# An S4-style block and a routed feed-forward block on one core: first routed query group moved into the light stage, index stores of the two routings spread, turning matrix and last stores rearranged

## The chip, the cores and the metric

The kernel runs on one core of a Trainium2 chip. The metric is the device time of one execution in microseconds (us). The engines are TensorE (PE, matrix products; PEld loads its weights), VectorE (DVE), ScalarE (ACT), GpSimd (POOL) and SyncE (SP). Each takes its own instructions in order; a DMA is issued from the instruction stream of one of them.

## The reference, cut to what matters

The input is x of shape (8, 2048, 512), float32. Two blocks with a skip connection follow each other:

```python
x = x + ssm(layernorm(x))      # per channel: causal convolution over the sequence,
                               # kernel K[d, l] = sum_n C*B_bar*A_bar**l, plus D*x
x = x + ffn(layernorm(x))

def ffn(x):
    light = light_attn(x)                     # windows of 64, own window and both neighbours
    sq,  iq  = route(x, rt_q,  512)           # 512 query rows of each sequence
    skv, ikv = route(x, rt_kv, 1024)          # 1024 context rows of each sequence
    out = heavy_attn(x[iq], x[ikv], skv)      # 8 heads of 64, rms norm, one null key
    full = broadcast(null_q); full[iq] = out * sq
    return light + full
```

`route` scores every row by a dot product, runs 50 rounds of coordinate descent and takes the top rows. All is float32.

## The kernel before, in words

The rows are 128 tiles of 128 rows, 16 to a sequence. There are three stages, one after the other on PE.

**Stage 1, `ssm_phase`.** The 512 channels are taken as 4 blocks of 128. The results of a block stay on chip (`xb`) and `store` writes them to the array `y`, one store per sequence b, each of 1 MB. The last block's stores cannot hide behind a further block: b = 0 goes out on POOL's queue, b = 1 to 7 on ACT's queue (line 353), and each is made to wait until the one before has landed (line 361, `stored[-1]`).

**Stage 2, `light_phase`.** 32 macro tiles of four row tiles. For the first macro tile the kernel already holds `z` on chip with the rows of each tile in reverse order; `turn(0)` turns them over and transposes them with one product against `flip`, a 128 by 128 matrix with ones on the other diagonal, which POOL makes (lines 721 to 724) with a memset and an affine select. `front(n)` makes the keys (`pp`, line 905; DVE evicts them, line 910), then the queries (evicted by ACT, line 908), then the values (line 918). The list of half steps in `steps()` is an order written out by hand for PE: 256 half steps, two to a row tile, each with scores (`sim`, line 974), exponentials on ACT (984), scaling on DVE (990), transposes (1000), the products `po` (1018), an ACT eviction `ot` (1022) and, once per row tile, the output product `pr` (1027), from which DVE makes `row` (1029) and POOL `nul` (1033). `rows`, `turn` and `front` of later macro tiles are generators of which a piece is run in every half step.

Beside this run the two routings, one for sequences 0 to 3 (group 0) and one for 4 to 7 (group 1). `route` is a generator too, and every half step runs two of its pieces through `between`. It has 144 pieces of arithmetic, then the 128 indirect stores of its results (line 641), two to a piece, then 16 pieces that load the lists back. The stores are queued on POOL behind the latest `nul`, so they run once per row tile (two half steps): eight together while one routing stores, sixteen while both do. Group 0 begins at half step 110 and stores from half step 182 to 213; group 1 begins at 132 and stores from 204 to 235.

**Stage 3, `heavy_phase`.** For each sequence three groups of 512 gathered rows: one of queries, two of keys and values. `fetch(n)` issues four gathers of group n (`xg`) from POOL's queue, `norm(n)` makes `z` from them (statistics on DVE, one power on POOL, line 1251, four scalings on DVE, line 1254), then come 16 transposes (line 1269), their evictions, and 16 products for the queries or keys (line 1286), with 16 more for the values. The heavy attention of a sequence also gathers the light result of its query rows, `bg` (line 1318 calls `gather`, line 1213), on POOL's queue.

Of the kernel before, what the change touches and what calls it, by code (L numbers as in the profile page):

```python
# [8 lines left out]
F32 = mybir.dt.float32  # L9
# [3 lines left out]
ALU = mybir.AluOpType  # L13
# [4 lines left out]
P = 128  # L18
B, L, D = 8, 2048, 512
# [4 lines left out]
NC = D // P  # L24
H, DH, WIN = 8, 64, 64
# [68 lines left out]
def ssm_phase(tc, k, x, log_A, B_param, C, Dp, ys):  # L94
# [10 lines left out]
    with ExitStack() as ctx:  # L105
# [245 lines left out]
        def store(cb, b):  # L351
            last = cb == NC - 1
            eng = nc.scalar if last and b else nc.gpsimd
            for y, c0 in ys[b]:
                c1 = c0 + y.shape[0] // P
                i = eng.dma_start(
                    y.rearrange("(i p) d -> p i d", p=P)[:, :, cb * P : (cb + 1) * P],
                    xbs[cb % 2][:, b * NCK + c0 : b * NCK + c1, :])
            if last:

                if b:
                    tc.add_manual_dep(i.ins, stored[-1].ins.name,
                                      mybir.DependencyInfo(mybir.DependencyClass.Sync,
                                                           mybir.DependencyReason.DATA),
                                      reason="stores in turn")
                stored.append(i)
# [107 lines left out]
def route(tc, k, ps, gi, flat, ix, wt):  # L474
# [160 lines left out]
    for r in range(2):  # L635
        nc.vector.tensor_copy(pair[:, r * GB * NCK : (r + 1) * GB * NCK, 0], rows)
    yield
    for b in range(GB):
        for rb, n in ((b, NQT), (GB + b, NLT)):
            for c in range(rb * NCK, (rb + 1) * NCK):  # L640
                nc.gpsimd.indirect_dma_start(  # L641
                    out=flat[c % NFL], out_offset=bass.IndirectOffsetOnAxis(ap=to[:, c : c + 1],
                                                                            axis=0),
                    in_=pair[:, c, :], in_offset=None, bounds_check=2 * GB * NKV - 1,
                    oob_is_err=False)
                if c % 2:
                    yield
    for b in range(GB):
        for rb, n in ((b, NQT), (GB + b, NLT)):
# [19 lines left out]
NM = L // MTOK  # L669


def light_phase(tc, k, ps, wp, args, x, ys, x1, base, out, between, after):

# [5 lines left out]
    with ExitStack() as ctx:  # L679
# [38 lines left out]

        xf = x.rearrange("b l d -> (b l) d")

        flip = sb.tile([P, P], F32, name="flip", tag="nul")
        nc.gpsimd.memset(flip, 0.0)
        nc.gpsimd.affine_select(flip, flip, [[1, P]], ALU.not_equal, 1.0, base=-(P - 1),
                                channel_multiplier=1)
# [207 lines left out]
        def keys(t):  # L932

            it, j = place(t)
            if t == NTT - 1:
                key = k.zp.tile([P, NC, 4 * WIN], F32, name="tail", tag="z")
                nc.gpsimd.memset(key[:, :, HALO:], 0.0)
                nc.gpsimd.tensor_copy(key[:, :, 0:HALO], it["k"][:, :, MTOK:])
                return key, 0
            return it["k"], P * j + P  # L940
# [108 lines left out]
        def steps():  # L1049
# [27 lines left out]
            for s in range(nst):  # L1077
# [3 lines left out]
                if s == 0 or j == 0:  # L1081
                    run(ahead)
                    run(turning)
                    run(scoring)
                    if n == FIRST - 2:
                        between(group=0)
                    if n == NMT - 1:
                        after()
                    ahead = front(n + 1) if n + 1 < NMT else None
                    beyond = rows(n + 2) if n + 2 < NMT else None  # L1090
                    turning = None
                    scoring = later(n - 2) if n in (2, 3) else None
# [12 lines left out]
                if j == 4 and n + 2 < FIRST:  # L1105
                    run(scoring)
# [15 lines left out]
                    done = t  # L1122
                run(ahead, 1)
            finish(done, ots.pop(done))
            between()

        with tc.manual_schedule(engines={mybir.EngineType.PE}):
# [32 lines left out]
    return ld  # L1160


def heavy_phase(tc, k, ps, wp, loaded, w_out, x1, base, out, lists):


# [6 lines left out]
    scale = DH**-0.5  # L1172
    with ExitStack() as ctx:

        inp = ctx.enter_context(tc.tile_pool(name="he_i", bufs=1, reuse_waits="tile"))
# [32 lines left out]
        groups = [(b, i) for b in range(B) for i in range(NG)]  # L1208
        xgs, zs = {}, {}

        def gather(src, ix, c, tag, bufs, pool=sb):
            t = pool.tile([P, D], F32, name=tag, tag=tag, bufs=bufs)
            nc.gpsimd.indirect_dma_start(
                out=t, out_offset=None, in_=src,
                in_offset=bass.IndirectOffsetOnAxis(ap=ix[:, c : c + 1], axis=0),
                bounds_check=B * L - 1, oob_is_err=False)
            return t

        def fetch(n):

            if n >= len(groups):
# [9 lines left out]
            xgs[n] = [gather(x1, ix, c0 + m, "xg", MT + 1, inp) for m in range(MT)]  # L1231

        def norm(n):

            if n >= len(groups):  # L1240
                return
            xg = xgs.pop(n)
            st = sb.tile([P, MT, 6], F32, name="st", tag="st")
            mv = sb.tile([P, MT, 2], F32, name="mv", tag="mv")
            rs = sb.tile([P, MT], F32, name="rs", tag="rs")
            for i in range(MT):
                nc.vector.bn_stats(st[:, i, :], xg[i])
                nc.vector.bn_aggr(mv[:, i, :], st[:, i, :])
            nc.vector.tensor_scalar(rs, mv[:, :, 1], EPS_LN, 1e-24 / D, ALU.add, ALU.mult)
            nc.vector.tensor_tensor(rs, rs, mv[:, :, 1], ALU.max)  # L1250
            nc.gpsimd.tensor_tensor(rs, rs, k.neghalf[:, :MT], ALU.pow)
            z = zs[n] = inp.tile([P, MT, D], F32, name="z", tag="z", bufs=1)
            for i in range(MT):
                nc.vector.tensor_scalar(z[:, i, :], xg[i], mv[:, i, 0:1], rs[:, i : i + 1],
                                        ALU.subtract, ALU.mult)

        def feed():

            fetch(0)
            norm(0)  # L1260
            fetch(1)
            for n, (b, i) in enumerate(groups):
                it = its[b]
                z = zs.pop(n)
                xt = sb.tile([P, NC, MT * P], F32, name="xt", tag="xt")
                for c in range(NC):
                    pt = ps["tp"].tile([P, MT * P], F32, name="pt", tag="tp")
                    for m in range(MT):
                        nc.tensor.transpose(pt[:, m * P : (m + 1) * P],
                                            z[:, m, c * P : (c + 1) * P], k.ident)  # L1270
                    if c % 2 == 0:
                        nc.vector.tensor_scalar(xt[:, c, :], pt, g[:, c : c + 1], None, ALU.mult)
                    else:
                        nc.scalar.mul(xt[:, c, :], pt, g[:, c : c + 1])
                    if c % 2:
                        yield b - 1
                if i == 0:
                    q = it["q"] = sb.tile([P, NC, NQ], F32, name="q", tag="q")
                elif i == 1:
                    kk = it["k"] = low.tile([P, NC, NKV], F32, name="kk", tag="kk")  # L1280
                ms = slice((i - 1) * MT * P, i * MT * P)
                for f in range(NC):
                    pp = ps["mm"].tile([P, MT * P], F32, name="pp", tag="mm")
                    for c in range(NC):
                        w = wq[:, c, :] if i == 0 else wkf[:, 0, c, :]
                        nc.tensor.matmul(pp, w[:, f * P : (f + 1) * P], xt[:, c, :],  # L1286
                                         start=c == 0, stop=c == NC - 1)
                    if i == 0:
                        nc.scalar.mul(q[:, f, :], pp, scale)
                    else:  # L1290
                        nc.vector.tensor_copy(kk[:, f, ms], pp)  # L1291
# [175 lines left out]
def model(ctx, tc, ins, out, debug=None):  # L1467
# [43 lines left out]
    def after():  # L1511
        loaded.update(heavy_loads(tc, wp, rms_g, w_q_h, w_kv_h, null_kv))

    light_phase(tc, k, ps, wp, (ln_g, ln_b, w_qkv, w_out_l, null_q, rt_q, rt_kv), x, ys, x1, base,
                outf, between, after)
    heavy_phase(tc, k, ps, wp, loaded, w_out_h, x1, base, outf, lists)


# [28 lines left out]
```

## Time and profile before

| | us |
|---|---|
| nine runs, median (lowest to highest) | 4871.77 (4866.91 to 4884.26) |
| profiled execution | 4873.9 |
| its span | 4872.2 |
| PE busy in it | 4517.6 (93%) |
| DVE, ACT, POOL busy in it | 2923.5, 1892.4, 1186.2 |
| last product of stage 1 ends, first product of stage 2 begins | 500.5, 515.0 |
| last product of stage 2 ends, first of stage 3 begins | 3151.5, 3163.2 |

The times of the trace count from the start of the span. A row of the timeline gives start, duration, engine, line, operation, tiles, how many instructions the row joins, and in square brackets for how long the engine had been idle before and what released it.

### The profile page before, as it was taken

How to read it: one execution, taken by the hardware profiler on the slowest of the kernel's cores; microseconds unless marked ns; L12 is line 12 of the kernel's file. 1: busy time of each engine (PE TensorE's matmuls, PEld its weight loads, DVE VectorE, ACT ScalarE, POOL GpSimd, SP SyncE). 2: the span in 40 equal slices, each digit the busy share in tenths (PEclk: the TensorE clock that was granted, in tenths of full speed). 3: DMA queues.
4: the chain of work that ended last, by engine and by line, in shares of the span. 5: the costliest groups of instructions: out<-in, count | busy, mean ns of one | idle time of the engine just before them, and what ended most of it. 6: DMA issues, size and time to landing. Idle time of an engine off the chain costs nothing.

```text
span 4872.2 us, 74936 instructions
## 1 busy us (share of the span) xinstructions
PE 4517.6 (93%) x28312; PEld 2628.0 (54%) x28312; DVE 2923.5 (60%) x6971; ACT 1892.4 (39%) x5069; POOL 1186.2 (24%) x1359
## 2 busy tenths in 40 slices
PE   1788899999999999999999899899999999999987
PEld 1677455555555555555554455445555555555554
DVE  8587578777777766668785344445444444454433
ACT  6988133333333333444332233323333333333333
POOL 5354222222222211000145575211101111011000
PEclk9999999999999999999999899999999999999998
DMA  7398634333333321111121122310000100000000
GB/s 255 113 242 222 204 114 141 115 122 117 122 116 119 109 94 58 62 48 57 49 57 42 38 55 53 88 41 27 31 18 27 31 27 27 22 27 27 12 12 12
DMA packets 270090, 383.96 MB, mean 79 GB/s; under 512 B 61728, under 2 KB 134688, under 8 KB 269728
## 3 DMA queue, kind: packets, MB, share of 16 engines
q1 hardware_dynamic: 214688, 268.45, 17.7%
q0 software_dynamic: 40464, 103.37, 7.3%
q10 hardware_dynamic: 14576, 7.34, 0.5%
q8 instruction: 223, 3.65, 0.3%
q14 instruction: 139, 1.14, 0.1%
HBM read 235.42 MB, written 143.72 MB: 78 GB/s over the span
## 4 chain that ended last, share of the span: by engine, by line
PE 56%; issue 27%; DMA 4%; DVE 2%; POOL 1%; another core or an unknown queue 1%; ACT 1%; POOLq 0%; DVEq 0%; ACTq 0%
PE pp L905 18%; PE pv L918 9%; PE pr L1027 9%; PE po L1018 5%; PE pt L1000 4%; PE sim L974 4%; DMA xg<-x,ix 2%; PE pt L886 1%; DMA y<-xb 1%; PE pv L1302 1%; DMA out_dram<-row,ix 1%; PE pp L1286 1%; PE sim L1337 1%; PE pt L1412 1%
## 5 line engine op out<-in xcount | busy, mean ns | idle before, releaser
L905 PE MATMUL pp<-xt,wqkv 128*128 128x512 f32 x2048 | 936.8, 601 | 0.2 <-ACT q L908 0.2
L905 PEld LDWEIGHTS pp<-xt,wqkv 128*128 128x128 f32 x2048 | 369.3, 190 | 398.2 <-issue 396.6
L1343 DVE TENSOR_REDUCE mx<-sim 128x1 f32<-128x1024 f32 x256 | 312.8, 1222 | 343.6 <-PE sim L1337 196.8
L984 ACT ACTIVATE pe<-sim,nb 128x256 f32<-128x256 f32 x1024 | 471.1, 473 | 51.0 <-DVE nb L979 47.3
L1027 PE MATMUL pr<-wo,ot 128*128 128x512 f32 x1024 | 470.4, 601 | 17.5 <-ACT ot L1022 15.4
L918 PE MATMUL pv<-wqkv,xt 128*128 128x512 f32 x1032 | 476.4, 605 | 3.1 <-issue 3.1
L1022 ACT COPY ot<-po 128x256 f32<-128x256 f32 x256 | 95.3, 372 | 978.7 <-PE po L1018 809.7
L1347 ACT ACTIVATE pe<-sim,nb 128x1024 f32<-128x1024 f32 x256 | 285.3, 1114 | 460.8 <-DVE nb L1344 455.1
L979 DVE TENSOR_REDUCE nb<-sim 128x4 f32<-128x1024 f32 x256 | 312.6, 1221 | 198.0 <-PE sim L974 113.5
L1033 POOL TENSOR_TENSOR nul<-row,nq 128x512 f32<-128x512 f32 x128 | 162.5, 1269 | 930.4 <-DVE row L1029 759.5
L1412 PE MATMUL pt<-ident,pe 128*128 128x128 f32 x2048 | 285.9, 284 | 89.6 <-ACT pe L1347 62.9
L1286 PE MATMUL pp<-xt,wa 128*128 128x512 f32 x768 | 351.3, 602 | 4.6 <-DVE kk L1291 4.6
L1412 PEld LDWEIGHTS pt<-ident,pe 128*128 128x128 f32 x2048 | 234.3, 144 | 173.0 <-ACT pe L1347 88.6
L1415 DVE COPY pw<-pt 128x512 f32<-128x512 f32 x256 | 175.6, 686 | 243.8 <-PE pt L1412 243.1
L1000 PEld LDWEIGHTS pt<-ident,pe 128*128 128x128 f32 x2048 | 239.8, 141 | 139.2 <-issue 138.9
L990 DVE TENSOR_SCALAR pe<-pe,rec 128x256 f32<-128x256 f32 x1024 | 298.3, 354 | 7.7
L918 PEld LDWEIGHTS pv<-wqkv,xt 128*128 128x128 f32 x1032 | 186.7, 190 | 210.8 <-issue 207.6
L1027 PEld LDWEIGHTS pr<-wo,ot 128*128 128x128 f32 x1024 | 186.7, 193 | 207.6 <-issue 186.4
L1018 PE MATMUL po<-pw,v 128*64 128x128 f32 x4096 | 282.8, 279 | 5.6 <-issue 5.1
L1417 ACT COPY pw<-pt 128x512 f32<-128x512 f32 x256 | 149.9, 585 | 349.1 <-PE pt L1412 349.1
L641 POOL DMA_INDIRECT list<-r_pair,r_to x256 | 254.4, 994 | 90.0 <-issue 71.5
L1000 PE MATMUL pt<-ident,pe 128*128 128x128 f32 x2048 | 268.8, 274 | 5.6 <-issue 5.6
(250 smaller groups left out, 7158.7 us busy)
## 6 DMA issues: line engine op xcount, KB each, us to landing
xin<-in_L_attn_x_dram SPq DMA_DIRECT2D x32, 1024.0 KB
x1t<-in_L_attn_x_dram SPq DMA_DIRECT2D x128, 256.0 KB
x<-x1t SPq DMA_DIRECT2D x128, 256.0 KB
x1r<-x SPq DMA_DIRECT2D x128, 256.0 KB
base<-row SPq DMA_DIRECT2D x128, 256.0 KB
out_dram<-nul SPq DMA_DIRECT2D x128, 256.0 KB
y<-xb POOLq DMA_DIRECT2D x21, 1024.0 KB
x1t<-x SPq DMA_DIRECT2D x72, 256.0 KB
```

The costliest lines, as they stand in the source:

```text
L905: nc.tensor.matmul(pp, wqkv[:, c, j * D + f * P : j * D + (f + 1) * P], xt[:, c, WIN:], start=c == 0, stop=c == NC - 1)
L918: nc.tensor.matmul(pv[0:m], xt[:, c, s * P : s * P + m], wqkv[:, c, 2 * D :], start=c == 0, stop=c == NC - 1)
L979: dve = nc.vector.reduce_max(nb, sim.rearrange("p a b c -> p (a b) c"), axis=AX.X, negate=True)
L984: act = nc.scalar.activation(pe[:, i, :], sim[:, i // 2, i % 2, :], AF.Exp, bias=nb[:, i : i + 1], accum_out=sums[:, i : i + 1])
L990: nc.vector.tensor_scalar(pe[:, i, :], pe[:, i, :], rec[:, i : i + 1], None, ALU.mult)
L1000: nc.tensor.transpose(pt[:, par, kb, :], self.pe[:, 2 * par + pr, kb * P : (kb + 1) * P], k.ident)
L1018: nc.tensor.matmul(po[64 * par : 64 * par + 64, pr, :], vs[kb][:, h * DH : (h + 1) * DH], self.pw[pr][:, par, kb, :], start=kb == 0, stop= ...
L1027: nc.tensor.matmul(pr, ot[:, c, :], wo[:, c, :], start=c == 0, stop=c == NC - 1)
L1286: nc.tensor.matmul(pp, w[:, f * P : (f + 1) * P], xt[:, c, :], start=c == 0, stop=c == NC - 1)
L1343: nc.vector.reduce_max(mx, sim[:, par, :], axis=AX.X, negate=True)
L1347: nc.scalar.activation(pe, sim[:, par, :], AF.Exp, bias=self.nb[:, h : h + 1], accum_out=self.sums[:, h : h + 1])
L1412: nc.tensor.transpose(pt[:, i, :], pes[half][:, kb * P : (kb + 1) * P], k.ident)
```

## The change

- `store`: the last block's store b waits for the one of b - 2, so that two are under way at a time (1 and 2 both wait for 0).
- `flip` is a tile of the pool `inp`, in a slot that the row tiles `x1t` use later, and no longer of the pool `sb`, in a slot of `nul`.
- `route`: group 0 yields after the third and the fifth of every five stores, so that five stores go out per half step (ten per row tile) and its 128 stores take some 26 half steps; group 1 yields as before. Group 1 starts four half steps later, at macro tile 17, j = 2 (half step 136), and so stores from 208 to 239; `sooner` still ends where it did.
- The first query group of sequence 0 (four gathers, norm, 16 transposes, four times four products) is taken out of `heavy_phase` and becomes `heavy_lead`, which runs in the light stage's last macro tile as `ahead`, the place that `front` has in the earlier ones: the gathers at its first half step, the products in its last. In half steps without `finish`, its piece is queued behind the transposes of the half step. Its queries stay in `k.q0`.
- `heavy_phase` begins with the gathers and the norm of group 1 and the gathers of group 2; the gathers of `bg` are queued on POOL behind the latest gathers of `xg`. The statistics of a norm share one tile. The key tile of the last row tile moves to the slot of `xt`.

```diff
-                    tc.add_manual_dep(i.ins, stored[-1].ins.name,
+                    tc.add_manual_dep(i.ins, stored[max(b - 2, 0)].ins.name,
...
+    stops = (2, 4) if gi == 0 else (1, 3)
...
-                if c % 2:
+                if c % (1 + stops[-1]) in stops:
                     yield
...
-        flip = sb.tile([P, P], F32, name="flip", tag="nul")
+        flip = inp.tile([P, P], F32, name="flip", tag="x1t", bufs=7)
...
-                key = k.zp.tile([P, NC, 4 * WIN], F32, name="tail", tag="z")
+                key = sb.tile([P, NC, 4 * WIN], F32, name="tail", tag="xt")
...
-                    ahead = front(n + 1) if n + 1 < NMT else None
+                    ahead = front(n + 1) if n + 1 < NMT else lead(inp, sb) if n < NMT else None
...
                 if n == FIRST and j == 6:
                     run(sooner)
+                if n == FIRST + 1 and j == 2:
                     between(group=1)
...
-                else:
-                    run(ahead, 1)
+                elif n < NMT - 1:
+                    run(ahead, 1)
+                else:
+                    with tc.issue_after(anchors[0].ins), tc.issue_after(anchors[1].ins):
+                        run(ahead, 1)
...
+def heavy_lead(tc, k, ps, loaded, x1, ix, inp, sb):
+    nc = tc.nc
+    xg = [gathered(nc, inp, x1, ix, m, "x1t", 7)[0] for m in range(MT)]
+    yield
+    yield
+    z = k.zp.tile([P, MT, D], F32, name="z", tag="z")
+    both_norms(nc, k, sb, xg, z, "junk", 1)
+    yield
+    yield
+    xt = sb.tile([P, NC, MT * P], F32, name="hxt", tag="xt")
+    yield from turned_rows(nc, k, ps, z, loaded["g"], xt)
+    q = k.q0 = k.zp.tile([P, NC, NQ], F32, name="q0", tag="z")
+    for f in range(NC):
+        queries(nc, ps, q, loaded["wa"][:, 0], xt, f)
+        yield
...
+            if n == 0:
+                it["q"] = k.q0
+                return
...
             fetch(0)
-            norm(0)
             fetch(1)
+            norm(1)
+            fetch(2)
             for n, (b, i) in enumerate(groups):
+                if n == 0:
+                    continue
...
-                self.bg = gather(base, self.it["ixq"], j, "bg", 2)
+                with tc.issue_after(its["last"].ins):
+                    self.bg, _ = gathered(nc, sb, base, self.it["ixq"], j, "bg", 2)
```

`gathered`, `both_norms`, `turned_rows` and `queries` hold the statements that `gather`, `norm` and `feed` had.

More of the change, by code (lines that the diff above doesn't have):

```diff
@@ L669, with light_phase @@
 NM = L // MTOK
-def light_phase(tc, k, ps, wp, args, x, ys, x1, base, out, between, after):
+def light_phase(tc, k, ps, wp, args, x, ys, x1, base, out, between, after, lead):
     nc = tc.nc
@@ L1124, in steps @@
             finish(done, ots.pop(done))
+            run(ahead)
             between()
@@ L1160, in heavy_loads, with gathered, both_norms @@
     return ld
+def gathered(nc, pool, src, ix, c, tag, bufs):
+    t = pool.tile([P, D], F32, name=tag, tag=tag, bufs=bufs)
+    i = nc.gpsimd.indirect_dma_start(
+        out=t, out_offset=None, in_=src,
+        in_offset=bass.IndirectOffsetOnAxis(ap=ix[:, c : c + 1], axis=0),
+        bounds_check=B * L - 1, oob_is_err=False)
+    return t, i
+def both_norms(nc, k, sb, xg, z, tag, bufs):
+    t = sb.tile([P, 9 * MT], F32, name="hst", tag=tag, bufs=bufs)
+    st = t[:, 0 : 6 * MT].rearrange("p (m s) -> p m s", s=6)
+    mv = t[:, 6 * MT : 8 * MT].rearrange("p (m s) -> p m s", s=2)
+    rs = t[:, 8 * MT :]
+    for i in range(MT):
+        nc.vector.bn_stats(st[:, i, :], xg[i])
+        nc.vector.bn_aggr(mv[:, i, :], st[:, i, :])
+    nc.vector.tensor_scalar(rs, mv[:, :, 1], EPS_LN, 1e-24 / D, ALU.add, ALU.mult)
+    nc.vector.tensor_tensor(rs, rs, mv[:, :, 1], ALU.max)
+    nc.gpsimd.tensor_tensor(rs, rs, k.neghalf[:, :MT], ALU.pow)
+    for i in range(MT):
+        nc.vector.tensor_scalar(z[:, i, :], xg[i], mv[:, i, 0:1], rs[:, i : i + 1],
+                                ALU.subtract, ALU.mult)
@@ new lines, in turned_rows, with queries @@
+def turned_rows(nc, k, ps, z, g, xt):
+    for c in range(NC):
+        pt = ps["tp"].tile([P, MT * P], F32, name="pt", tag="tp")
+        for m in range(MT):
+            nc.tensor.transpose(pt[:, m * P : (m + 1) * P], z[:, m, c * P : (c + 1) * P], k.ident)
+        if c % 2 == 0:
+            nc.vector.tensor_scalar(xt[:, c, :], pt, g[:, c : c + 1], None, ALU.mult)
+        else:
+            nc.scalar.mul(xt[:, c, :], pt, g[:, c : c + 1])
+        if c % 2:
+            yield
+def queries(nc, ps, q, wq, xt, f):
+    pp = ps["mm"].tile([P, NQ], F32, name="pp", tag="mm")
+    for c in range(NC):
+        nc.tensor.matmul(pp, wq[:, c, f * P : (f + 1) * P], xt[:, c, :], start=c == 0,
+                         stop=c == NC - 1)
+    nc.scalar.mul(q[:, f, :], pp, DH**-0.5)
@@ new lines, in heavy_lead @@
+def heavy_lead(tc, k, ps, loaded, x1, ix, inp, sb):
[12 more added lines that the diff above has]
+        queries(nc, ps, q, loaded["wa"][:, 0], xt, f)
+        yield
@@ L1171, in heavy_phase @@
     wq, wkf = loaded["wa"][:, 0], loaded["wa"][:, 1:3]
-    scale = DH**-0.5
     with ExitStack() as ctx:
@@ L1209, in heavy_phase @@
         xgs, zs = {}, {}
[L1211 to L1217, printed above, removed]
         def fetch(n):
@@ L1230, in fetch @@
             ix, c0 = (it["ixq"], 0) if i == 0 else (it["ixk"], (i - 1) * MT)
-            xgs[n] = [gather(x1, ix, c0 + m, "xg", MT + 1, inp) for m in range(MT)]
-        def norm(n):
[L1240 to L1255, printed above, removed]
+            if n == 0:
+                it["q"] = k.q0
+                return
@@ L1257, in feed @@
+            got = [gathered(nc, inp, x1, ix, c0 + m, "xg", MT + 1) for m in range(MT)]
+            xgs[n] = [t for t, _ in got]
+            its["last"] = got[-1][1]
+        def norm(n):
+            if 0 < n < len(groups):
+                z = zs[n] = inp.tile([P, MT, D], F32, name="z", tag="hz", bufs=1)
+                both_norms(nc, k, sb, xgs.pop(n), z, "hst", 2)
         def feed():
             fetch(0)
-            norm(0)
             fetch(1)
+            norm(1)
+            fetch(2)
@@ L1262, in feed @@
             for n, (b, i) in enumerate(groups):
+                if n == 0:
+                    continue
                 it = its[b]
-                z = zs.pop(n)
                 xt = sb.tile([P, NC, MT * P], F32, name="xt", tag="xt")
[L1266 to L1272, printed above, removed]
-                    else:
-                        nc.scalar.mul(xt[:, c, :], pt, g[:, c : c + 1])
-                    if c % 2:
-                        yield b - 1
+                for _ in turned_rows(nc, k, ps, zs.pop(n), g, xt):
+                    yield b - 1
@@ L1277, in feed @@
                 if i == 0:
-                    q = it["q"] = sb.tile([P, NC, NQ], F32, name="q", tag="q")
+                    it["q"] = sb.tile([P, NC, NQ], F32, name="q", tag="q")
                 elif i == 1:
@@ L1282, in feed @@
                 for f in range(NC):
[L1283 to L1287, printed above, removed]
                     if i == 0:
-                        nc.scalar.mul(q[:, f, :], pp, scale)
+                        queries(nc, ps, it["q"], wq, xt, f)
                     else:
+                        pp = ps["mm"].tile([P, MT * P], F32, name="pp", tag="mm")
+                        for c in range(NC):
+                            nc.tensor.matmul(pp, wkf[:, 0, c, f * P : (f + 1) * P], xt[:, c, :],
+                                             start=c == 0, stop=c == NC - 1)
                         nc.vector.tensor_copy(kk[:, f, ms], pp)
@@ L1512, in after, with lead @@
         loaded.update(heavy_loads(tc, wp, rms_g, w_q_h, w_kv_h, null_kv))
+    def lead(inp, sb):
+        return heavy_lead(tc, k, ps, loaded, x1, lists[0][0][:, 0], inp, sb)
     light_phase(tc, k, ps, wp, (ln_g, ln_b, w_qkv, w_out_l, null_q, rt_q, rt_kv), x, ys, x1, base,
-                outf, between, after)
+                outf, between, after, lead)
     heavy_phase(tc, k, ps, wp, loaded, w_out_h, x1, base, outf, lists)
```

## The prediction

> **What bounds the kernel.** I read the engines' busy shares first, then a table of busy time by stretches of the span, then the timeline where PE is not full.
>
> ```profile
> span 4872.2 us, 74936 instructions
> PE 4517.6 (93%) x28312; PEld 2628.0 (54%) x28312; DVE 2923.5 (60%) x6971; ACT 1892.4 (39%) x5069; POOL 1186.2 (24%) x1359
> ```
>
> ```profile
> 2560.00:2630.00 70.00, 70.00 (x404) 37.47 (x402) 48.16 (x151) 22.63 (x76) 31.87 (x33) 1.00 0.23 51
> 2630.00:2780.00 150.00, 118.70 (x580) 59.52 (x582) 44.58 (x90) 33.59 (x111) 85.75 (x88) 0.85 0.14 34
> 2780.00:2990.00 210.00, 210.00 (x1236) 112.87 (x1228) 95.73 (x193) 69.29 (x230) 139.05 (x174) 1.00 0.23 50
> ```
>
> In the second table the columns are the stretch, its length, busy PE, PEld, DVE, ACT and POOL, PE's granted clock, the share of the DMA engines and GB/s. PE is the bound: 93% of the span, all of it in most of stage 2. The change alters little of PE's work, so it is worth what it takes out of PE's gaps, and each is read in its own place: 14.5 us between stages 1 and 2, 2630 to 2780, and 11.7 us between stages 2 and 3.
>
> **Turning matrix and last stores.**
>
> ```profile
> 508.94 35.11 ACTq L356 DMA_DIRECT2D y<-xb  x7
> ...
> 514.62 0.31 POOL L723 TENSOR_SCALAR_AFFINE_SELECT flip<-flip 128x128 f32<-128x128 f32 x1
> ...
> 514.99 5.57 PE L883 MATMUL pt<-flip,z 128*128 128x128 f32 x32 [14.49 <-POOL flip L723]
> ...
> 544.18 1.57 ACT L908 ACTIVATE q<-pp 128x512 f32<-128x512 f32 x3 [54.32 <-DMA y<-xb]
> ```
>
> PE ends stage 1 at 500.5 and waits for `flip`, which POOL makes behind four gathers that wait for a store. The other operand, `z`, is there at 508.44 (506.52 + 1.92 of the scalings, line 782). With `flip` in a slot that is free early, its two instructions (0.23 and 0.31 us) run before that, in the idle time of POOL, and PE starts 0.3 behind `z` as it starts 0.06 behind `flip` now: at about 508.8, 6.2 us earlier.
>
> Alone this is worth nothing. ACT stands at the seven stores, each of which waits for the landing of the one before, until 544.18; PE has run ahead of it as far as the buffers for `pp` go and loses only 0.24 us there now (the product at 544.83). Started 6.2 us earlier, it would stop at the same place and wait until 544.8. From 522.54 on a store takes 5.05 to 5.80 us from issue to landing, one after the other, with the DMA engines 0.74 busy from 525 to 535. So two at a time can bring a store down to 5.05 x 0.74 = 3.7 us and no further; seven then take some 26 to 30 us from 508.9, the last waits for the fifth, and ACT is free at about 528 to 532, before the 538 at which PE, 6.2 earlier, needs it. Both together: 6.2, plus the 0.24 and up to a few tenths at DVE's statistics, which wait 12.28 us for the same stores at 549.13. I take **7**. Bounds: 0 (a pair is no faster than one after the other) and 10 (PE's waits of 2.44 and 3.91 at 566 and 572 shrink too; the latter is for one `sim` buffer, which the change leaves).
>
> **The index stores.**
>
> ```profile
> L641 POOL DMA_INDIRECT list<-r_pair,r_to x256 | 254.4, 994 | 90.0 <-issue 71.5 <-DMA list<-r_pair,r_to 17.8 <-DMA r_got<-list 0.3
> ```
>
> ```profile
> 2509.42 0.37 ACT L1022 COPY ot<-po 128x256 f32<-128x256 f32 x1 [2.90 <-PE po L1018]
> 2524.54 0.37 ACT L1022 COPY ot<-po 128x256 f32<-128x256 f32 x1 [6.58 <-PE pt L1000]
> ...
> 2659.89 0.37 ACT L1022 COPY ot<-po 128x256 f32<-128x256 f32 x1 [3.08 <-PE po L1018]
> 2683.12 0.37 ACT L1022 COPY ot<-po 128x256 f32<-128x256 f32 x1 [18.59 <-remote]
> ...
> 2683.55 3.78 PE L1027 MATMUL pr<-wo,ot 128*128 128x512 f32 x4 [6.94 <-ACT ot L1022]
> ```
>
> A store takes 0.98 us of POOL and 0.30 to the next, 1.28. From 2630 to 2770 both routings store, and POOL has five bursts of 16, each about 20.3 us (2660.31 to 2680.6, say). In each one `ot` stands until 1.6 to 2.7 us behind the burst's last store, with a releaser that the trace can't name (remote): 13.95, 18.59, 14.22, 14.82, 10.31 us. PE waits for `ot` and, in between, issues slowly. The loss is read from the starts of `sim`: an undisturbed half step is 9.77 us, or 10.64 where a piece of `front` more is in it, and from 2629.01 to 2779.52 two half steps each took 28.93, 29.32, 29.75 and 30.87 us, and one 20.99, instead of 20.4, 19.5, 19.5, 20.4 and 9.8. (A macro tile later, with one routing storing, the same places show the lower numbers; one more half step at 2747.88 is undisturbed.) That is 8.5 + 9.8 + 10.2 + 10.5 + 11.2 = **50 us**. The starts of `pv` agree: one macro tile takes 118.9 us (2630.85 to 2749.72) instead of 80, and holds four of the five.
>
> Bursts of eight, 10 us each, cost next to nothing: group 0's eleven from 2410 to 2623 shift the half steps by 0.8 us in all; group 1's from 2785 on, by 0. But they too hold `ot` up: two evictions are 9.77 us apart, so the one at 2524.54 is 5.35 late against 2509.42 + 9.77. Over the eleven the lateness is 2.3, 2.3, 0, 2.7, 3.5, 5.35, 0.3, 2.8, 3.2, 5.35, 0.4. It is covered because PE has other products between. How much is covered: at least 5.1 (5.35 late cost 0.2 to 0.46), or, from the burst of 16 in the rows above, 13.46 late - 9.77 lost = 3.7.
>
> After the change the two groups overlap no more (182 to 207, 208 to 239), and group 0 has 128 / 10 = 12.8 bursts of ten, 12.6 us long: each holds `ot` 2.57 us longer than a burst of eight. Adding 2.57 to each lateness that is over 2 and taking off 5.1 leaves 7.8 us for eleven, 0.7 a burst; taking off 3.7 leaves 18.6, 1.7 a burst. I take the middle, 1.2, as both covers are seen: 12.8 x 1.2 = **15 us** (9 to 22; far ends 0 and 9.9 a burst as for 16). Group 1's 16 bursts of eight run where its routing has ended and cost 0 as now. The later start of group 1 moves its arithmetic four half steps on and its lists to half step 248, still ahead of stage 3, which reads them for the fifth sequence. Net: 50 - 15 = **35**.
>
> **The first query group.**
>
> ```profile
> 3158.96 1.08 POOL L1213 DMA_INDIRECT bg<-base,ix  x1 [4.87 <-DMA base<-row]
> ...
> 3161.39 1.06 POOL L1251 TENSOR_TENSOR rs<-rs,neghalf 128x4 f32<-128x4 f32 x1
> ...
> 3163.18 4.45 PE L1269 MATMUL pt<-ident,z 128*128 128x128 f32 x16 [11.68 <-DVE z L1254]
> 3167.47 13.90 PE L1286 MATMUL pp<-xt,wa 128*128 128x512 f32 x32
> ```
>
> PE ends stage 2 at 3151.50. DVE's statistics end at 3156.13, but the power waits 5.3 us behind two `bg` gathers, which wait for a store. Then PE spends 18.0 us on group 0 (3163.18 to 3181.21), 31.6 on group 1, 30.6 on group 2: 91.9 to 3243.44.
>
> After: the `bg` gathers come behind the `xg` gathers, so the power of group 1's norm follows its statistics at 3156.1 and PE's gap is 3156.1 + 1.06 + about 0.8 to the first transpose - 3151.5 = 6.5 (near 0 if this norm is moved ahead of the last row's work on DVE; its gathers are there, as the same ones land by 3000 now). Then 31.5 + 30.6: 68.6 in all, 23.3 less. Group 0's 18 us do not vanish: they go into stage 2's last 65 us, where PE waits in only a few places (1.32, 1.51, 1.32, 1.97 at 3105 to 3138). Behind the lead's products three of these, 4.8 us, can be filled; 13.2 are added. DVE gets 5.8 us there (four statistics of 0.66 + 0.17, 0.3, four scalings of 0.54), in a tail paced by the softmax; I put 2 on the path. The four gathers (1.3 us each) lie on POOL, idle 9.86 us before its `nul` at 3145.18. Net 23.3 - 15.2 = **8**. Bounds: -3 (nothing filled, DVE wholly on the path: 23.3 - 18 - 5.8, and some waits kept) and 14 (the gap goes). The merged statistics tile and the moved key tile change no instruction's length: 0, unless a slot is freed late, and the slots they take were last read in the macro tile before.
>
> **Sum.** 7 + 35 + 8 = 50 off the profiled execution's 4873.9: 4824. That execution is 2.1 above the median of the runs, 4871.8, so the forecast is **4822**.
>
> **Rivals.**
>
> 1. *Bursts of ten are covered as those of eight.* For it: only two of eleven bursts of eight come near the cover. Against: 5.35 + 2.57 is beyond either. It gives 15 more: 4807. Chance 0.24.
> 2. *Slower: bursts of ten stall like those of 16.* The mechanism is `ot` held to the end of a burst with PE out of other products. If the cover were used up at once, as the slow issue inside the bursts of 16 hints (gaps of 0.4 to 1.8 us from 11 us after the first store), 12.8 bursts x 9.9 = 127 lost against 50 + 15 saved: 62 more than before, 4934. It decides from 65 / 12.8 = 5.1 us a burst on. Against: 5.1 is beyond 2.57 longer plus what eight cost. Chance 0.08.
> 3. *The stalls do not come from POOL's stores.* The five half steps with two routings would stall for another reason, and spreading the stores gives 0: 7 + 8 = 15 off, 4857. Against: five stalls in five bursts, each ending some 2 us behind its burst, none from 2780 on with one routing storing. Chance 0.08, half of it below 0.2% with a poor lead. The Trainium skill, page "SBUF — State Buffer", section "Who interferes with whom", says that PE and ACT never wait on anyone, since only the port pair of DVE and GpSimd is shared. By that rule no burst on POOL could hold up `ot` through the memory, and the sum would be this rival's; the row of 18.59 us at 2683.12 speaks for a wait of another kind, which the rule doesn't exclude.
> 4. *The lead is a wash.* Its 18 us and DVE's work lengthen the tail by as much as the start of stage 3 gains: 0 to -5 in place of 8, 4830 to 4835. Chance 0.15.
>
> The forecast has the rest, 0.45. Range for 8 in 10: below, free bursts with the gap gone and 3 more at the stores, 4822 - 15 - 6 - 3 = 4798; above, 2.5 us a burst (17 more), the lead a wash (8) and 3 at the stores (4): 4851. A measurement of this kernel tells 0.2%, 9.7 us, from no change: faster 0.45 + 0.24 + 0.15 + 0.04 = 0.88, same 0.04, slower 0.08.
>
> **What the profile after would show.** Right: the first product with `flip` at about 508.8 and no wait of PE for `q`; bursts of ten, then of eight, never of 16; no `ot` held for over 9 us; half steps of group 0's stores longer by 0.7 to 1.7 in one of two; first transposes of stage 3 about 6.5 us after the last `pr`. Wrong: a wait of PE for `q` near 540 (pairs no faster), `ot` held 13 us in bursts of ten (rival 2), stalls where no store runs (rival 3), PE waits in the last 65 us of stage 2 that are as many as now or more (rival 4).

## The result, and the profile after

The changed kernel takes 4850.32 us (median of 11 runs, 4835.76 to 4857.81) against 4872.77 for the kernel before (34 runs). The ratio is 0.9954 (95% interval 0.9945 to 0.9962): 22 us faster, where 50 were forecast. The profiled execution took 4848.2 us, its span is 4846.5, which is 25.7 less than the 4872.2 before.

The page's head and the table by stretches of the changed kernel answer to the first lines shown of before:

```profile
span 4846.5 us, 74937 instructions
...
PE 4519.9 (93%) x28312; PEld 2631.4 (54%) x28312; DVE 2924.9 (60%) x6971; ACT 1892.3 (39%) x5069; POOL 1185.9 (24%) x1359
```

```profile
2560.00:2630.00 70.00, 65.97 (x382) 33.84 (x381) 52.39 (x200) 20.09 (x67) 36.26 (x37) 1.00 0.16 43
2630.00:2780.00 150.00, 150.00 (x877) 81.33 (x876) 78.60 (x180) 49.40 (x165) 108.46 (x148) 1.00 0.30 52
```

The stretch with the two routings' bursts is full now (150.00 of 150, 118.70 before). The one ahead of it, where group 0 stores alone, was full and has lost 4 of 70.

**Where the time went.** The same half step has a `sim` in both traces, and the same row tile of stage 3 a `row`. The start in the one less the start in the other shows what has been gained up to there. I write down where this number moves:

| part of the span | gained so far | change |
|---|---|---|
| stage 1 to half step 3 of stage 2 | 8.8 | +8.8 |
| group 0's stores (half steps 187 to 208) | -8.1 | -16.8 |
| where both groups stored before (208 to 217) | 41.1 | +49.1 |
| half steps 231 and 239, group 1's stores | 28.4 | -12.7 |
| last eight half steps of stage 2 | 16.0 | -12.4 |
| to the first `row` of stage 3 | 36.2 | +20.2 |
| from there to row 25 of stage 3 | 19.5 | -16.7 |
| last rows of stage 3 | 25.6 | +6.1 |

The first three rows are the forecast's first two parts: 8.8, -16.8 and 49.1 where 7, -15 and 50 were forecast, 41 us together in place of 42. The rest is the lead. Its forecast was 8 us; up to row 25 it is -21.6. Two of its rows were in no step of the forecast: the stalls at half steps 231 and 239, and the loss inside stage 3.

**Stalls in group 1's stores.** This is the first, from the timeline of the changed kernel:

```profile
2866.42 1.06 POOL L1174 DMA_INDIRECT x1t<-x,ix  x1 [0.31 <-issue]
...
2871.97 0.70 DVE L1193 BATCH_NORM_STATS2 hst<-x1t 128x6 f32<-128x512 f32 x1 [8.82 <-DMA x1t<-x,ix]
2872.58 0.67 DVE L1010 COPY pw<-pt 128x512 f32<-128x512 f32 x1
...
2873.31 1.12 PE L1021 MATMUL po<-pw,v 128*64 128x128 f32 x8 [4.60 <-DVE pw L1010]
```

The lead's code stands in the last macro tile, at 3050 or so, but only PE's order is written out by hand. The scheduler put the lead's gathers and statistics as far ahead as their slots and queues let it, 180 us early, between index stores. The slots of `x1t` come free one by one, so the gathers trickle out: one at 2866, two at 2875, the last at 2952. DVE takes its queue in order, and the first statistics (`hst`) stand there for 8.82 us, with the `pw` behind them that PE needs. At 2957.65 the fourth statistics wait 7.30 us in the same way.

**Loss inside stage 3.** These are the rows around one of the row tiles that took 55.1 to 55.5 us instead of 52.5, in the changed kernel:

```profile
4182.56 1.00 POOL L1174 DMA_INDIRECT xg<-x,ix  x1 [0.30 <-issue]
4183.87 1.00 POOL L1174 DMA_INDIRECT bg<-base,ix  x1 [0.30 <-issue]
4185.18 1.00 POOL L1174 DMA_INDIRECT xg<-x,ix  x1 [0.30 <-DVE hst L1193]
...
4188.52 1.09 PE L1462 MATMUL pt<-ident,pe 128*128 128x128 f32 x8 [0.98 <-ACT pe L1397]
4188.88 0.69 DVE L1193 BATCH_NORM_STATS2 hst<-xg 128x6 f32<-128x512 f32 x1 [1.73 <-DMA xg<-x,ix]
...
4191.11 0.68 DVE L1340 COPY kk<-pp 128x512 f32<-128x512 f32 x1
...
4191.85 5.40 PE L1338 MATMUL pp<-xt,wa 128*128 128x512 f32 x8 [2.23 <-DVE kk L1340]
```

A `bg` gather has come between the third and the fourth `xg` gather. The fourth goes out 1.3 us later, DVE waits 1.73 for it, the eviction of the keys behind it is late, PE waits 2.23, and then eight products take 5.40 us in place of 3.70. Before, the `bg` gather went out first, 7.7 us ahead of the four, in idle time of POOL.

Most of the loss is of the second kind. From the first row of stage 3 to row 25 PE is busy for 1229.2 us instead of 1216.7, with the same products: 12.5 of the 16.7 us are products that ran longer. The granted clock (PE's clock as a share of full speed, in the profile) is 0.59 from 4191.85 to 4195.50. From the first row to row 25 it stands at half for 47.8 us in the changed kernel and for 20.5 before.

### The profile page after: what moved, and what is told of

It is laid out like the page before. It is cut to its first block, busy times and chain, and to the rows that moved or that the text cites. A ratio compares the mean times of both kernels' runs of the same rounds, so it can differ in the third digit from the quotient of the medians.

```text
span 4846.5 us, 74937 instructions
## 1 busy us (share of the span) xinstructions
PE 4519.9 (93%) x28312; PEld 2631.4 (54%) x28312; DVE 2924.9 (60%) x6971; ACT 1892.3 (39%) x5069; POOL 1185.9 (24%) x1359
## 3 DMA queue, kind: packets, MB, share of 16 engines
q1 hardware_dynamic: 214688, 268.45, 17.6%
## 5 line engine op out<-in xcount | busy, mean ns | idle before, releaser
L1387 PE MATMUL sim<-kk,q 64*128 64x512 f32 x1024 | 265.7, 639 | 0.0
```

The costliest lines, as they stand in the source:

```text
L1387: nc.tensor.matmul(sim[:, par, ms], q[rows_, f, self.qs], kk[rows_, f, ms], start=True, stop=True)
```

## The experiments

Each ran beside the kernel before on the same chip; "us" is the median of the runs. The kernel before took 4868.70 to 4873.47 us beside them and 4872.77 beside the changed kernel, so a difference between two kernels that ran beside different ones of these is uncertain by up to 5 us for that alone; the ratios are free of it.

| kernel | us | ratio to before, 95% interval |
|---|---|---|
| flip_only | 4871.02 | 1.0006 (0.9996 to 1.0015) |
| stores_only | 4867.35 | 0.9996 (0.9985 to 1.0007) |
| spread_only | 4835.98 | 0.9926 (0.9912 to 0.9940) |
| lead_only | 4906.01 | 1.0066 (1.0052 to 1.0079) |
| no_lead | 4826.83 | 0.9905 (0.9890 to 0.9920) |
| bg_free | 4832.75 | 0.9917 (0.9903 to 0.9930) |
| lead_pinned | 4847.84 | 0.9947 (0.9933 to 0.9960) |
| eights | 4837.23 | 0.9925 (0.9911 to 0.9938) |
| lead_early | 4806.26 | 0.9878 (0.9859 to 0.9896) |
| eights_no_lead | 4819.06 | 0.9898 (0.9879 to 0.9917) |
| twelves | 4841.30 | 0.9933 (0.9917 to 0.9948) |
| sixteens | 4871.24 | 0.9996 (0.9981 to 1.0011) |

### Turning matrix and stores, each alone

`flip_only`: the kernel before with

```diff
-        flip = sb.tile([P, P], F32, name="flip", tag="nul")
+        flip = inp.tile([P, P], F32, name="flip", tag="x1t", bufs=7)
```

> The kernel before with the turning matrix in its new slot and nothing else. Theory (ACT stands at the stores one after the other until 544, so PE comes to the same wait earlier): the first product of stage 2 starts at about 509, PE then waits some 6 us for the queries' eviction, and the time is as before, 4872, within 2 us. Rival (the matrix alone brings its 6 us, the stores bring nothing): 4866.

`stores_only`: the kernel before with

```diff
-                    tc.add_manual_dep(i.ins, stored[-1].ins.name,
+                    tc.add_manual_dep(i.ins, stored[max(b - 2, 0)].ins.name,
```

> The kernel before with the last block's stores two at a time and nothing else. Theory: PE still starts stage 2 at 515 for want of the turning matrix, only the 0.2 us at the queries and up to 1 us at DVE go: 4871. Rival (pairs let the gathers ahead of the matrix land earlier or later and move the start by some us): the first product of stage 2 away from 515 by over 1 us.

Neither moves the time by more than the interval. `flip_only` shows why, in its timeline:

```profile
507.60 6.00 PE L883 MATMUL pt<-flip,z 128*128 128x128 f32 x32 [6.64 <-DVE z L782]
509.18 36.03 ACTq L356 DMA_DIRECT2D y<-xb  x7
...
545.41 1.58 ACT L908 ACTIVATE q<-pp 128x512 f32<-128x512 f32 x3 [55.02 <-DMA y<-xb]
546.06 5.46 PE L905 MATMUL pp<-xt,wqkv 128*128 128x512 f32 x8 [8.42 <-ACT q L908]
```

PE starts 7.4 us earlier and gives it all back at 546, waiting 8.42 us for ACT, which still stands at the stores. In the changed kernel, with both edits, the stores are issued by 534.5 and the wait is gone:

```profile
506.97 6.72 PE L886 MATMUL pt<-flip,z 128*128 128x128 f32 x32 [6.64 <-DVE z L785]
508.56 25.95 ACTq L356 DMA_DIRECT2D y<-xb  x7
...
534.72 1.08 ACT L911 ACTIVATE q<-pp 128x512 f32<-128x512 f32 x2 [44.97 <-PE pp L908]
```

ACT's idle time there ends with PE's products now, no longer with a DMA. In `stores_only` the first product with `flip` still has a gap of 14.51 us in front of it; it begins at 512.02 because that execution's stage 1 was shorter. From there to the first `sim` it took 48.5 us against 51.7, so the stores alone may bring up to 3 us; the medians (1.4 us apart) do not settle that.

### The index stores

`spread_only` is the kernel before with the change's edits of `route` and of group 1's start:

```diff
+    stops = (2, 4) if gi == 0 else (1, 3)
...
-                if c % 2:
+                if c % (1 + stops[-1]) in stops:
...
-                    between(group=1)
+                if n == FIRST + 1 and j == 2:
+                    between(group=1)
```

> The kernel before with the index stores of the two routings apart (bursts of ten, then of eight) and nothing else. Theory (50 us of bursts of 16 go, 15 to 19 of bursts of ten come): 31 to 35 faster than before, 4836 to 4840. Rival (part of the 50 is lost to the two routings and comes back elsewhere): under 25 faster, 4847 or more.

It is 37.5 us faster than before. Its half steps lose 15.2 us under group 0's stores and gain 49.1 where both groups stored, 34 together: the theory. Its last six rows of stage 3 gain 6.1 more, which are no part of the edit (last section).

`eights` is the changed kernel with

```diff
-    stops = (2, 4) if gi == 0 else (1, 3)
+    stops = (1, 3)
...
-                if n == FIRST + 1 and j == 2:
+                if n == FIRST + 2 and j == 0:
```

> The changed kernel with bursts of eight for both groups and group 1 started ten half steps later than before (half step 142), so that the groups still do not overlap. Theory (the loss in group 0's stores, 16.8 us in the profile, is the length of a burst over what covers ot): it falls to 0 to 2 us, 4834. Rival (the loss comes of two routings at work, whatever the length of a burst): under 5 us gained, 4846 or more.

13 us faster than the changed kernel. The loss under group 0's stores is 0.2 us instead of 16.8, with as much routing arithmetic beside it; the rival falls. The profiled execution, the slowest of its five, is only 3.6 us faster than that of the changed kernel, mostly because it is 2.2 us behind at the start of stage 2, loses 2.3 more at half steps 240 and 241, and loses 22.2 us inside stage 3 instead of 16.7.

`twelves` and `sixteens` start from `lead_early` (below), which has bursts of eight, and lengthen group 0's alone:

```diff
-    stops = (1, 3)
+    stops = (2,) if gi == 0 else (1,)      # twelves
...
+    stops = (3,) if gi == 0 else (1,)      # sixteens
```

> The version with bursts of eight and the mended lead (4806), with bursts of twelve for group 0 alone. Theory (a burst holds ot to its end, 1.28 us a store, and PE pays what is over a cover of 3.7 to 5.1 us): 2.5 to 4 us a burst, 10.7 bursts, 27 to 43 us more, 4833 to 4849. Rival (a threshold between ten and sixteen, below it 1.3 us a burst): 4820.

> The same with bursts of sixteen for group 0, which has them to itself, since group 1 starts later. Theory (the length alone counts): 9 to 10 us a burst as in the kernel before, eight bursts, 72 to 80 us more, 4878 to 4886. Rival (it was the meeting of two routings, with their arithmetic on DVE and two lists): well under half of that, below 4846.

They take 35 and 65 us more than `lead_early` (30 and 60 by the differences to the kernel before). For `twelves` that is the theory; `sixteens`, at 4871, lies below its theory and far above its rival. The table by stretches shows it for 2375 to 2640, in `lead_early`, the changed kernel, `twelves` and `sixteens`, in this order:

```profile
2375.00:2640.00 265.00, 265.00 (x1538) 143.93 (x1537) 187.61 (x627) 96.27 (x330) 116.34 (x117) 1.00 0.23 54
```

```profile
2375.00:2640.00 265.00, 253.52 (x1444) 133.79 (x1444) 183.27 (x657) 83.89 (x288) 129.64 (x131) 0.99 0.20 49
```

```profile
2375.00:2640.00 265.00, 243.54 (x1342) 127.65 (x1342) 159.03 (x517) 83.30 (x294) 138.57 (x139) 0.96 0.17 45
```

```profile
2375.00:2640.00 265.00, 225.45 (x1207) 117.01 (x1206) 137.87 (x441) 73.70 (x259) 151.13 (x158) 0.92 0.16 39
```

PE's busy time falls as POOL's rises, and the granted clock (the third number from the end) falls with it, from 1.00 to 0.92: a part of the price is products that run slowly. From the half steps, the mean loss of a burst is:

| stores in a burst | loss under group 0's stores | bursts | us a burst |
|---|---|---|---|
| 8 (`eights`) | 0.2 | 16 | 0.0 |
| 10 (changed kernel) | 16.8 | 12.8 | 1.3 |
| 12 (`twelves`) | 32.0 | 10.7 | 3.0 |
| 16 (`sixteens`) | 59.1 | 8 | 7.4 |
| 16, both groups (before) | 50 | 5 | 10.0 |

The mean price rises steadily from some eight stores on, and 1.3 and 3.0 lie inside what the cover model gave (0.7 to 1.7, 2.5 to 4). For sixteen alone it gave too much. But these are means over uneven bursts. The trace of the changed kernel has bursts of 8 to 12 stores. One of twelve, from 2486 on, costs 6.3 of the 16.8 us, another, from 2602 on, 2.6: where a burst falls in PE's order counts too. In `sixteens` only the first three bursts stand apart; the next three and the last two run into one another (48 stores from 2480.6 to 2549.8, 32 from 2565.7 to 2612.0). So 7.4 is not the price of a single burst of sixteen, and whether the meeting of two routings adds a part of its own to the 10.0 of before is not shown.

### The lead

`no_lead` is the changed kernel's first two parts on the kernel before, that is `flip_only`, `stores_only` and `spread_only` together.

> The kernel before with the turning matrix, the paired stores and the spread index stores, but without the lead and with stage 3 as it was. Theory (the lead and the new queue order of stage 3 cost more than they bring: 12.7 us of waits of DVE for the lead's gathers, 12.4 in the tail and 16.7 in stage 3 against 20.2 at its start): about 22 us faster than the changed kernel, 4828. Rival A (the 16.7 us in stage 3 are chance and come without the new order too): 5 faster, 4845. Rival B (the lead is worth its 8 us as forecast): 8 slower, 4858.

`lead_only` is the changed kernel with those three edits taken back.

> The kernel before with the lead and the new queue order of stage 3 alone; turning matrix, stores and index stores as before. Theory (12 to 13 us of statistics that wait, 12 in the tail and 10 to 17 in stage 3 against 20 to 22 at its start): 13 to 20 slower than before, 4884 to 4891. Rival A (the forecast: the lead brings 8): 4863. Rival B (without the spread index stores the lead's gathers find another place and the statistics do not wait): 4872 to 4879.

`no_lead` is 24 us faster than the changed kernel (22 by the differences to the kernel before): the lead and the new order of stage 3 cost that much. `lead_only` is 33 us slower than before, more than the theory's 20. All of its terms are there, and two are larger, the waits of the statistics and the loss inside stage 3: it loses 16.6 us in half steps 231 and 239 (DVE's statistics wait 10.70 and 8.91 us there) and 12.4 in the last eight, gains 20.0 at the start of stage 3, and loses 23.7 from its first row to its 25th.

`bg_free` is the changed kernel with

```diff
-                with tc.issue_after(its["last"].ins):
+                with tc.issue_after(its["last"].ins) if b == 0 else nullcontext():
```

> The changed kernel, with the bg gathers of sequence 0 alone queued behind the xg gathers, and those of the other sequences where the scheduler puts them, as before. Theory (a bg gather between the third and the fourth xg gather makes DVE wait for the fourth, the keys late and PE idle long enough to run slowly after it): the row tiles of stage 3 that took 55.1 to 55.5 us take 52.5, and the kernel is 10 to 17 us faster than the changed one, about 4836. Rival (those tiles are slow by chance): as the changed one, 4850, with as many tiles of 55.

17.6 us faster than the changed kernel. The gathers around the same row tile go out in the old order, and PE's wait is a third:

```profile
4165.88 1.03 POOL L1174 DMA_INDIRECT bg<-base,ix  x1 [0.31 <-issue]
4173.60 1.07 POOL L1174 DMA_INDIRECT xg<-x,ix  x1 [6.70 <-DVE z L1199]
...
4184.47 3.70 PE L1338 MATMUL pp<-xt,wa 128*128 128x512 f32 x8 [0.76 <-DVE kk L1340]
```

From the first row to row 25 the granted clock stands at half for 20.5 us here, as in the kernel before. That it is the order and not chance is seen across the runs: from the first row of stage 3 to the 25th the four kernels with the new order lose 15.6 to 23.7 us against before; the other nine, with the old one for all sequences or all but the first, lie between 2.5 lost and 5.9 gained.

`lead_pinned` is the changed kernel with all of the lead queued behind its own half step:

```diff
-                run(ahead, 1)
+                with ExitStack() as held:
+                    if n >= NMT - 1:
+                        for i in list(anchors) + last:
+                            held.enter_context(tc.issue_after(i.ins))
+                    run(ahead, 1)
```

> The changed kernel, with every piece of the lead queued behind the instructions of its own half step on POOL, DVE and ACT, so that its gathers and statistics cannot be put in front of earlier half steps. Theory (the statistics stand in DVE's queue in front of pw and wait for gathers that trickle out one by one): the two stalls of 7.3 and 5.4 us in group 1's stores go, 4838. Rival (the waits only move to the last half steps, where PE has nothing else): 4848 to 4852, with waits of PE for DVE in the last 60 us of stage 2.

The rival was right. The two stalls are gone (40.9 us gained up to half step 249, as against 28.4), but the last half steps lose 25.8 us instead of 12.4. The gathers now go out at 3066.85, behind list loads, and the statistics wait for them where PE has nothing else to do:

```profile
3072.42 0.69 DVE L1197 BATCH_NORM_STATS2 hst<-x1t 128x6 f32<-128x512 f32 x1 [5.23 <-DMA x1t<-x,ix]
```

```profile
3079.40 1.12 PE L1021 MATMUL po<-pw,v 128*64 128x128 f32 x8 [7.05 <-DVE pw L1010]
```

So what costs most is not where the statistics stand, but that they stand in front of data that has not landed.

### The version that follows

`lead_early` takes `eights`, `bg_free`, and a lead whose gathers go out together once the slots are free (half step 240) and whose statistics come three half steps behind:

```diff
-                    ahead = front(n + 1) if n + 1 < NMT else lead(inp, sb) if n < NMT else None
+                    ahead = front(n + 1) if n + 1 < NMT else leading if n < NMT else None
...
+                if n == NMT - 2 and j in (2, 5):
+                    if j == 2:
+                        leading = lead(inp, sb)
+                    with ExitStack() as held:
+                        for i in list(anchors) + last:
+                            held.enter_context(tc.issue_after(i.ins))
+                        run(leading, 1 if j == 2 else 2)
...
     both_norms(nc, k, sb, xg, z, "junk", 1)
-    yield
-    yield
+    for _ in range(5):
+        yield
```

> The changed kernel with bursts of eight for both groups, the bg order of all sequences but the first as before, and the lead's gathers together at half step 240 and its statistics three half steps later, both queued behind their own half step. Theory (three separate costs: 15 us of bursts of ten, 16 of the bg order in stage 3, 12.7 of statistics that wait for gathers): all three go and nothing comes in their place, 4850 - 44 = 4806. Rival (the statistics cost PE as much wherever they stand): 4816 to 4820.

`eights_no_lead` is `no_lead` with the edits of `eights`:

> The kernel before with the turning matrix, the paired stores and bursts of eight for both groups (group 1 from half step 142), without the lead and with stage 3 as before. Theory (bursts of ten cost 19 us in the run without the lead, those of eight nothing): 4827 - 17 = 4810, and some 5 us behind the version with a mended lead, whose start of stage 3 saves 21 us and whose tail costs 12. Rival (the later lists of group 1 lengthen the end of stage 2): 4815 to 4825.

`lead_early` is the fastest, 4806.26 us, 44 less than the changed kernel (40 by the differences to the kernel before), as the sum of the three costs said. The gathers and statistics of its lead, in its timeline:

```profile
2984.93 1.06 POOL L1181 DMA_INDIRECT x1t<-x,ix  x1 [0.15 <-issue]
...
3010.70 1.28 DVE L1200 BATCH_NORM_STATS2 hst<-x1t 128x6 f32<-128x512 f32 x2
```

No wait stands in front of the statistics. They are not free even so: half steps 244 to 247 lose 4.1 us (about 5 in `twelves` and `sixteens`, which have the same lead). And inside stage 3 up to row 25 this execution is 5.9 us faster than the kernel before, with the granted clock at half for 10.2 us instead of 20.5; `twelves` and `sixteens`, with the same code there, lose 0.2 and 2.5. So the sum of 44 came out in part by luck: the statistics brought less than their 12.7, and a good execution of stage 3 made up for it.

`eights_no_lead` came out at 4819, which is the rival's number but not its reason: the end of stage 2 is as long as before (56.8 gained at half step 231, 56.7 at the last one), and its half steps under group 0's stores lose nothing. Against `no_lead` the two traces differ by 20 us at the end of stage 2, the medians by 8; its runs spread from 4808 to 4828, so how much of the 20 it keeps stays open. The mended lead is then worth about 13 us by the medians (4819 - 4806, on the same chip). In the traces its own places show 17 lost in stage 2 and 23 gained at the start of stage 3, 6 in all; 7 more come between the first row and row 25, where nothing of the lead runs.

## Why the prediction failed at the lead and held for the rest

**Turning matrix and stores: right.** 7 forecast, 8.8 measured, and neither part is worth anything clear alone, as forecast for the matrix. Counted from the end of stage 1 it is 8.6 in the changed kernel and 5.7 to 7.4 in the eight others with both edits. PE starts at 506.97 rather than 508.8, since it needs only the first of the four scalings of `z`.

**Index stores: right in both terms, but not in their spread.** 50 gained against 49.1; 15 lost against 16.8 in the changed kernel, and 14.7 to 19.4 in the five kernels with bursts of ten. The model of lateness and cover carried over to the mean of bursts of twelve. Rival 1 (bursts of ten are covered) and rival 2 (they cost as those of 16) both fall, and so does rival 3: with the bursts spread, the stalls went. One sign misled: `ot` was not to be held for over 9 us, and 13 was to speak for rival 2, but it was held for 15.09 in the burst of twelve, and for 10.94 and 9.03 in others. Nor did each second half step lose 0.7 to 1.7 us; two of them (6.3 and 2.9) hold more than half of the 16.8. PE and ACT lose 1.3 to 10.0 us a burst of more than eight stores in these traces. The rule that rival 3 leaned on (the Trainium skill, page "SBUF — State Buffer", section "Who interferes with whom": PE and ACT never wait on anyone) is about the ports of the memory. It gives no guide to the time here, but no run shows it broken either: what came late are signals of PE (last section).

**The lead: the step that failed.** Forecast +8, measured -21.6 up to the last rows, -22 to -24 by the runs with and without it. The step took it that the lead's gathers and statistics would run where their code stands, and that the new queue order of `bg` acts at the start of stage 3 alone. By its terms:

- "Net 23.3": the start of stage 3 gained 20.2. The gap is 6.49 us where 6.5 was forecast; the two groups behind it take 65.8 instead of 62.1, with waits of PE of 1.62 and 1.15 for the keys. Nearly right.

```profile
3131.83 3.70 PE L1030 MATMUL pr<-wo,ot 128*128 128x512 f32 x8
3142.02 4.57 PE L1208 MATMUL pt<-ident,z 128*128 128x128 f32 x16 [6.49 <-DVE z L1199]
```

- "13.2 are added": the last eight half steps lose 12.4. Right. The "2 on the path" for DVE were not put to the test there, since the lead's work on DVE had run before. With these two terms alone the lead would be worth 20.2 - 12.4 = 7.8, the forecast's 8.
- "DVE gets 5.8 us there", in the tail, and "the four gathers lie on POOL, idle": wrong. I took the place in the code for the place in the queues. The gathers went out 100 to 180 us earlier and the statistics waited for them, 12.7 us. The question of what is queued behind a new wait was not put to the lead's statistics.
- "The `bg` gathers come behind the `xg` gathers": counted at the start of stage 3 alone, where it helps. The same edit moves the `bg` gathers of all other sequences too, and there it costs 16.7 us, three quarters of it in products that ran longer. I had priced the first sequence's and not the 28 gathers of the others.

Rival 4, the lead as a wash, had the sign of this but neither the size nor the place: it gave 0 to -5 and saw the loss in the tail, which came out as forecast. That 4850 still lies at the upper end of the range, 4851, is luck: the range reached there by dearer bursts and a lead of 0, and neither is what happened. The last 6.1 us are no part of the change; see below.

## What to carry to other kernels

Where only one engine's order is written by hand, a moved step goes to where the others' queues will take it: find it there in the trace, and look at what stands behind its first wait. An instruction that waits for a gather should come so late that the gather has landed, and the gather so early that its slot is the only condition; pinning both to one place only moves the wait. An edit made for a stage's start is to be priced at every later place where the same line runs.

## What the runs showed of the hardware

- `ot` waits for PE alone in the program, and PE's product for it ends at 2493.47, yet it stood until the burst of index stores was over. ACT was idle for 15.09 us in one burst, which runs from 2486.12 to 2501.4 with twelve stores:

```profile
2503.47 0.37 ACT L1025 COPY ot<-po 128x256 f32<-128x256 f32 x1 [15.09 <-remote]
```

  The trace also records the updates of semaphores, the signals by which one engine releases another. From 2350 to 2400 each update by PE stands 0.01 to 0.05 us behind the end of its product. In this burst the products that give an update end at 2491.64, 2492.45, 2493.47, 2497.10, 2497.54 and 2497.98; the record, in which some updates are missing, has one at 2496.20 and the next four from 2503.45 to 2503.66. DVE's and ACT's own updates that are on record there stand 0.01 to 0.02 us behind their instructions. The burst of the kernel before from 2660 on shows the same (PE's products end from 2663.48 to 2674.13, the updates come at 2671.77 and from 2683.10 to 2683.31). So it is PE's signal that comes late. While `ot` stood in that burst (2664 to 2683), the DMA engines moved 1 GB/s, so it is not bandwidth. On average the longer burst is the dearer one (table above); what holds PE's signals stays open.
- In stage 3 of the changed kernel, waits of PE of 2.0 to 2.2 us are followed at five places by eight products of 5.2 to 5.4 us instead of 3.70: the late gather costs about 1.5 us as a wait (2.23 in place of 0.76) and as much again in slower products. They are slow by the clock: the granted clock is 0.59 from 4191.85 to 4195.50, and 1.00 at the same products of `bg_free` (4184.5 to 4188). It is not the one wait alone: in each of these places another of about 1 us lies 1.1 us of work before it (0.98 and 2.23 in the rows above). In the kernel before the one place with such products (5.12 us at 3806) has 2.80 and then 0.76. Where both waits together were 1.84 (1.08 and 0.76 in `bg_free`), the products took 3.70. The Trainium skill, page "TensorE: Matmul & The Clock Gate", section "What's actually happening", has the clock fall after an idle window of about 3.4 us that runs freely. No single wait here was that long; the traces agree only if such waits are added up over a short piece of work (3.0 to 3.6 us), which no run tests by itself.
- The last six rows of stage 3 take 5 to 6 us less in `no_lead`, `spread_only` and `stores_only` than before, and no less in `flip_only` and `eights_no_lead`, though in none of these five the code of stage 3 differs from before. The changed kernel's last 6.1 us are of this kind; a single profile can't tell a gain of that size from it.
